# A two-layer graph network on one core: nodes sorted in two groups, queue orders written out by hand

## Chip, core and metric

The kernel runs on one core of a Trainium2 chip. The metric is the device time of one execution in microseconds; nine executions of the kernel before gave a median of 1124.33 us (1121.89 to 1130.77).

The core's engines have a queue each and work through it in order: PE (matrix products), DVE (vector operations), ACT (pointwise functions and scaling), POOL (here almost only DMAs with row indices: gathers and scatters) and SP (plain DMAs).

## The reference

3327 nodes with 512 values each, and an adjacency matrix `adj` of zeros and ones, symmetric, with ones on the diagonal and about 9 neighbours per node. Two layers, each followed by a residual sum and a normalisation of every row:

```python
# layer 0: four heads of 128 columns
feats = einsum('nf,hfo->hno', x, W);  e_s = feats . a_self;  e_n = feats . a_neigh
logits = leaky(e_s[:, :, None] + e_n[:, None, :], 0.2), masked by adj
x = layernorm(x + relu(softmax(logits) @ feats + b))
# layer 1
attn_a = sigmoid(concat[adj @ x, x] @ Wa.T + ba);  attn_b = the same with Wb, bb
h = x @ W_sa
e = where(adj, exp(-leaky(h . a_left + (h . a_right)^T, 0.01)), 0)
x_a = (e / (sum(e) + 1e-5)) @ h
x_b = adj @ (x @ W_gcnb) + b_gcnb
x = layernorm(x + sigmoid(attn_a * x_a + attn_b * x_b))
```

## The kernel before

The matrix has few ones, so the kernel turns it into lists of neighbours and gathers rows. Nodes are handled in tiles of 128 (one per partition), 26 tiles in all. `sparse_pass` does the work; `dense_pass` is a fall-back that a flag calls if a list overflows, and isn't entered here.

**Stage 1, features and lists (lines 129 to 346).** A loop runs over seven chunks of 512 columns (the last has 256). SP loads the chunk of `x` transposed (L213) and the chunk of the matrix in seven loads of up to 1 MB (L218, ten buffers). PE makes the features of each tile (L227, 16 matmuls); ACT copies them out (L232 to L234), POOL writes them to `table0` in DRAM (L235). PE also multiplies the matrix by powers of two (L241, 52 matmuls per chunk), which packs 16 matrix rows into one number; DVE adds the block's number (L247, L250), PE transposes (L256), and DVE finds the largest 24 entries of each node by rounds of eight (`top8`, L50 and L53), takes the bits out in four levels (L261 to L281), sorts them by `top8` again and writes lists and degrees (L285 to L296).

After the last chunk, all nodes are ranked by degree (L301 to L328): a one-hot matrix of degrees, two products with PE, a running sum on DVE. POOL scatters the 26 list tiles to their sorted places (L330), SP loads them back as `srt` (L331). `CAPS` holds how many slots each sorted tile needs: 253 in all, from 23 down to 5.

**Stage 2, layer 0 (L411 to L479).** For each sorted tile `attend` gathers the tile's own rows of `x` (`xg`, L415) and then one row of `table0` for each slot (L382: one POOL instruction gathers 128 rows of 520 numbers). DVE and ACT make the softmax weights (L422 to L437). Each slot's rows are scaled in place, two thirds of the slots by DVE (L446), one third by ACT in four pieces (L444), and PE adds them up by a product with the unit matrix (L451, two instructions per slot). After each group of four tiles the rows are normalised, and `publish` transposes them on PE (L460), makes six columns (L465) and scatters the rows to `table1` (L467). This stage is ordered by a scheduler.

**Stage 3, layer 1 (L482 to L634).** The order is written out by hand: iteration `i` gathers tile `i + 3`, sums tile `i` (weighted on DVE, L544; plain on PE, L561, with some pairs added first by DVE, L546), projects tile `i - 1` (L579) and finishes tile `i - 2`; results are scattered to `out`. Eight gather buffers of six slots.

Every gather and scatter is a POOL instruction, and POOL works strictly in the order of its queue. Layer 0's gathers need `srt` and all of `table0`; layer 1's need all of `table1`.

Of the kernel before, what the change touches and what calls it, by code (L numbers as in the profile page):

```python
# [8 lines left out]
F32 = mybir.dt.float32  # L9
# [11 lines left out]

S = 24
CAPS = (23, 15, 14, 13, 12, 12, 11, 11, 10, 10, 10, 10, 9, 9, 9, 8, 8, 8, 8, 7, 7, 7, 6, 6, 5, 5)
LW = 32
ND = 32
LEVELS = 4
U = 15
U1 = 6
NCOL = 6
# [17 lines left out]
def top8(nc, pool, dst, src, width, tag, i):  # L47

    for r in range(S // 8):
        nc.vector.max(dst[:, 8 * r : 8 * r + 8], src)  # L50
        if 8 * (r + 1) < S:
            rest = pool.tile([P, width], F32, tag=f"top{tag}", name=f"top{tag}{i}_{r}", bufs=3)
            nc.vector.match_replace(rest, dst[:, 8 * r : 8 * r + 8], src, 0.0)  # L53
            src = rest
# [3 lines left out]
def sparse_pass(  # L58
# [27 lines left out]

    nc = tc.nc
# [5 lines left out]
    assert len(CAPS) == NT and NP == N + 1  # L93
    HC = F // 2 + H
    ROW = F + 2 * H

    const = ctx.enter_context(tc.tile_pool(name="const", bufs=1))
# [3 lines left out]
    lists = dram.tile([NP, LW], I32, name="lists")  # L101

    ident = const.tile([P, P], F32, name="ident")
    make_identity(nc, ident)
    ones = const.tile([P, P], F32, name="ones")
    nc.vector.memset(ones, 1.0)
    bias0 = const.tile([P, F], F32, name="bias0")
    nc.scalar.dma_start(bias0, row_bcast(b0, F))
    bias_g = const.tile([P, F], F32, name="bias_g")
    nc.scalar.dma_start(bias_g, row_bcast(b_g, F))  # L110
    bias_ab = const.tile([P, 2], F32, name="bias_ab")
    nc.scalar.dma_start(bias_ab[:, 0:1], row_bcast(ba, 1))
    nc.scalar.dma_start(bias_ab[:, 1:2], row_bcast(bb, 1))

    srt = const.tile([P, NT, LW], I32, name="srt")
    valid = const.tile([P, NT, S], F32, name="valid")
    v1 = const.tile([P, KT, NCOL], F32, name="v1")

    def scatter(group, dst, rows, src, last=None):
# [6 lines left out]
        tc.add_to_no_dep_group(group, put)  # L126


    with tc.tile_pool(name="p0", bufs=1) as p0, tc.tile_pool(name="p0s", bufs=2) as p0s:

        pow2 = p0.tile([P, 4, 32], F32, name="pow2")
        nc.gpsimd.memset(pow2, 0.0)
        pq = p0.tile([P, 8], I32, name="pq")
        nc.gpsimd.iota(pq, pattern=[[-16, 8]], base=0, channel_multiplier=1)
        inside = p0.tile([P, 8], F32, name="inside")
        nc.vector.tensor_scalar(inside, pq, 0, None, ALU.is_ge)
        upto = p0.tile([P, 8], F32, name="upto")
        nc.vector.tensor_scalar(upto, pq, 15, None, ALU.is_le)
        nc.vector.tensor_mul(inside, inside, upto)
        nc.vector.tensor_scalar(pq, pq, 127, None, ALU.add)  # L140
        nc.vector.tensor_scalar(pq, pq, 23, None, ALU.logical_shift_left)
        for s in range(4):
            nc.vector.tensor_mul(pow2[:, s, 8 * s : 8 * s + 8], inside, pq.bitcast(F32))

        pid = p0.tile([P, 4], I32, name="pid")
        nc.gpsimd.iota(pid, pattern=[[0, 4]], base=0, channel_multiplier=1)
        nc.vector.tensor_scalar(pid[:, 1:2], pid[:, 0:1], 7, None, ALU.bitwise_and)
        nc.vector.tensor_scalar(pid[:, 2:3], pid[:, 0:1], 5, 3, ALU.logical_shift_right, ALU.logical_shift_left)
        nc.vector.tensor_scalar(pid[:, 3:4], pid[:, 0:1], 3, 3, ALU.logical_shift_right, ALU.bitwise_and)
        nc.vector.tensor_scalar(pid[:, 3:4], pid[:, 3:4], 5, None, ALU.logical_shift_left)  # L150
# [917 lines left out]
```

## Time and profile before

The profiled execution took 1128.11 us, of which the span from first to last instruction is 1126.4 us.

| from the page | PE | DVE | ACT | POOL |
|---|---|---|---|---|
| busy, us | 840.0 | 718.0 | 225.9 | 657.9 |
| share of the span | 75% | 64% | 20% | 58% |

| stage | from, us | to, us | ended by |
|---|---|---|---|
| features and lists | 0 | 208 | ranks on DVE |
| lists sorted, loaded back | 208 | 250 | first gather of `table0` |
| layer 0 | 250 | 683 | last scatter to `table1`, then the first gather of it |
| layer 1 | 683 | 1126 | last scatter to `out` |

How to read it: the engines' lines give busy time in each stretch; a POOL gather is "busy" only while POOL writes its descriptors, and the rows land some 3.8 us after the issue (the page's part 6). PEclk is the TensorE clock that was granted, as a share of full speed; the DMA share is the mean busy share of the core's 16 DMA engines. "Issue" as the end of an idle stretch means that nothing in the profile shows what ended it.

### The profile page before, as it was taken

What the parts mean: (1) busy time and instruction counts of PE and PEld (TensorE: products, weight loads), DVE (VectorE), ACT (ScalarE), POOL (GpSimd) and SP (SyncE); (2) the same over time, 40 slices, a digit from 0 to 9 for tenths busy, and PEclk for the clock granted to TensorE, in tenths of its full rate; (3) what the DMA queues carried; (4) which work ended last, traced back from release to release, by engine and by line L of the source; (5) the groups of instructions that cost most, each with busy time, mean ns of one, the idle gap of its engine ahead of it and who ended that gap; (6) DMA issues with size and microseconds to landing.
All of it is one profiled execution on the core that took longest, in us unless ns stands there. A gap on an engine that the chain in (4) does not pass through costs nothing. (4 is left out here: it accounts for less than half of the span.)

```text
span 1126.4 us, 10006 instructions
## 1 busy us (share of the span) xinstructions
PE 840.0 (75%) x2662; PEld 427.0 (38%) x2662; DVE 718.0 (64%) x2103; ACT 225.9 (20%) x665; POOL 657.9 (58%) x689
## 2 busy tenths in 40 slices
PE   2999992100897595869867764969898999999981
PEld 0765561000333442425333441424443444444440
DVE  3499889200646355464657543378799898888771
ACT  0111110000423222233222320101212113132321
POOL 3310000457777677777777725777677777777411
PEclk9999996555798598986897885968999999999996
DMA  9999990028777667676767617777667676767400
GB/s 284 392 394 394 394 321 19 7 46 199 219 213 201 177 197 210 198 209 181 211 190 204 198 52 223 197 203 195 184 182 196 186 193 191 195 191 194 139 29 31
DMA packets 87809, 220.71 MB, mean 196 GB/s; under 512 B 17056, under 2 KB 23360, under 8 KB 87744
## 3 DMA queue, kind: packets, MB, share of 16 engines
q0 software_dynamic: 49664, 162.66, 51.1%
q1 hardware_dynamic: 34288, 54.69, 13.6%
q10 hardware_dynamic: 3792, 2.63, 0.8%
q8 instruction: 24, 0.39, 0.1%
q14 instruction: 41, 0.34, 0.1%
HBM read 198.85 MB, written 21.09 MB: 195 GB/s over the span
## 5 line engine op out<-in xcount | busy, mean ns | idle before, releaser
L382 POOL DMA_INDIRECT g<-table,srt x506 | 520.1, 1028 | 165.0 <-issue 138.9
L451 PE MATMUL acc<-g,ident 128*128 128x512 f32 x506 | 255.8, 663 | 88.4 <-DVE g L446 82.2
L561 PE MATMUL acc<-g,ident 128*128 128x512 f32 x378 | 183.3, 624 | 27.5 <-issue 15.2
L451 PEld LDWEIGHTS acc<-g,ident 128*128 128x128 f32 x506 | 104.3, 213 | 223.5 <-issue 140.8
L544 DVE SCALAR_TENSOR_TENSOR sw<-g,e,sw 128x512 f32<-128x512 f32 x227 | 170.2, 750 | 5.8
L446 DVE TENSOR_TENSOR g<-g,w 128x512 f32<-128x512 f32 x178 | 114.3, 692 | 0.7
L227 PE MATMUL pf<-w,xc 128*128 128x260 f32 x416 | 99.6, 394 | 18.7 <-DVE w L194 18.7
L579 PE MATMUL po<-wsa,sT 128*128 128x512 f32 x208 | 100.3, 628 | 15.2 <-ACT sT L572 15.2
L561 PEld LDWEIGHTS acc<-g,ident 128*128 128x128 f32 x378 | 69.6, 199 | 102.8 <-issue 70.6
L422 DVE TENSOR_TENSOR w<-g,srt 128x40 f32<-128x40 f32 (+10 forms) x27 | 5.4, 200 | 152.2 <-DMA g<-table,srt 115.3
L444 ACT ACTIVATE g<-g,w 128x128 f32<-128x128 f32 x300 | 90.5, 388 | 24.1 <-DVE w L437 19.4
L579 PE MATMUL po<-wg,sT 128*128 128x512 f32 x208 | 94.8, 599 | 0.7 <-ACT sT L572 0.7
L227 PEld LDWEIGHTS pf<-w,xc 128*128 128x128 f32 x416 | 79.1, 195 | 36.9 <-DVE w L194 20.5
L235 POOL DMA_DIRECT2D table<-row x26 | 14.1, 544 | 123.6 <-ACT st L234 113.7
L579 PEld LDWEIGHTS po<-wsa,sT 128*128 128x128 f32 x208 | 41.1, 201 | 70.9 <-issue 48.8
L433 ACT ACTIVATE w<-w 128x40 f32<-128x40 f32 (+11 forms) x26 | 6.1, 235 | 303.8 <-DVE w L432 261.5
L572 ACT COPY sT<-pt 128x512 f32<-128x512 f32 x52 | 30.0, 576 | 162.8 <-PE pt L570 162.8
L579 PEld LDWEIGHTS po<-wg,sT 128*128 128x128 f32 x208 | 39.9, 193 | 51.6 <-issue 47.4
L121 POOL DMA_INDIRECT out<-za,srt x26 | 27.0, 1038 | 52.8 <-ACT za L633 46.0
L121 POOL DMA_INDIRECT lists<-st,ranki x26 | 25.3, 972 | 42.9 <-DVE ranki L328 35.3
L121 POOL DMA_INDIRECT table<-x1s,srt x26 | 27.8, 1069 | 35.7 <-ACT x1s L466 29.1
L546 DVE TENSOR_TENSOR g<-g 128x512 f32<-128x512 f32 x64 | 44.3, 692 | 2.2
(152 smaller groups left out, 851.0 us busy)
## 6 DMA issues: line engine op xcount, KB each, us to landing
at<-in_adjT SPq DMA_DIRECT2D x36, 1024.0 KB, 15.3
g<-table,srt POOLq DMA_INDIRECT x506, 3.8
table<-row POOLq DMA_DIRECT2D x26, 260.0 KB, 5.7
xc<-in_xT SPq DMA_DIRECT2D x6, 1024.0 KB, 14.1
at<-in_adjT SPq DMA_DIRECT2D x12, 512.0 KB, 13.3
w<-in_W SPq DMA_DIRECT2D x4, 256.0 KB, 8.1
wsa<-in_W_sa ACTq DMA_DIRECT2D x1, 1024.0 KB, 12.4
wsa<-in_W_sa SPq DMA_DIRECT2D x1, 1024.0 KB, 6.0
```

Source lines behind the costliest of these rows:

```text
L121: put = nc.gpsimd.indirect_dma_start(out=dst, out_offset=bass.IndirectOffsetOnAxis(ap=rows, axis=0), in_=src, in_offset=None, bounds_check ...
L227: nc.tensor.matmul(pf[:, hh, :HC], xc[:, k, (t - t0) * P : (t - t0 + 1) * P], w0[:, k, hh, :], start=(k == 0), stop=(k == KT - 1),)
L235: nc.gpsimd.dma_start(table0[t * P : (t + 1) * P, :], row)
L382: nc.gpsimd.indirect_dma_start(out=g[:, s - s0, :], out_offset=None, in_=table[:, :], in_offset=bass.IndirectOffsetOnAxis(ap=srt[:, j, s : ...
L444: nc.scalar.activation(gv[:, h, :], gv[:, h, :], AF.Copy, scale=w[:, s, h : h + 1])
L446: nc.vector.tensor_tensor(gv, gv, w[:, s, :].rearrange("p (h o) -> p h o", o=1).to_broadcast([P, H, FO]), ALU.mult,)
L451: nc.tensor.matmul(acc, ident, g[:, s - s0, 0:F], start=(s == 0), stop=(s == c - 1))
L544: nc.vector.scalar_tensor_tensor(sw, g[:, i, 0:F], e[:, s : s + 1], sw, ALU.mult, ALU.add)
L546: nc.vector.tensor_add(g[:, i, 0:F], g[:, i - 1, 0:F], g[:, i, 0:F])
L561: nc.tensor.matmul(plain[j], ident, row, start=(not paired and i == 0), stop=(last and i == len(rows) - 1))
L572: nc.scalar.copy(sT, pt)
L579: nc.tensor.matmul(proj[j], sT[:, k, :], wt[:, k, :], start=(half + k == 0), stop=(half + k == KT))
```

## The change

The nodes are put in two groups: the first 12 tiles (three chunks of columns) and the last 14. Each group is ranked, scattered, loaded back and capped by itself; the two lists of slots add up to 126 and 144. The first group's lists are made along with the features of the first 20 tiles, then it is sorted and the remaining features follow. The second group's lists are cut into pieces (`yield`), and layer 0's loop runs three pieces in each of its iterations, between the two halves of the next tile's softmax weights; then come its rank, 14 scatters and the load. The whole of `sparse_pass` is now under a schedule written by hand.

In layer 0 each iteration gathers two tiles ahead, and a tile is normalised and published in four steps that lie in four successive iterations. The bias is added by PE (one more product per tile), the own rows of `x` are gathered into `x1` (12 at once before the first group, then one per tile), the mask of empty slots is replaced by a row of -1e30 in `table0`. The chunks of `x` are loaded by ACT's queue, the matrix by SP in 14 loads of up to 512 KB per chunk with 10 buffers. Block numbers are added by ACT. Both layers share seven gather buffers of six slots. Layer 1 has the same steps with another order of tiles (long and short in turn).

```diff
-CAPS = (23, 15, 14, 13, 12, 12, 11, 11, 10, 10, 10, 10, 9, 9, 9, 8, 8, 8, 8, 7, 7, 7, 6, 6, 5, 5)
+NG = (12, 14)
+CAPS = (23, 14, 12, 11, 10, 10, 9, 9, 8, 7, 7, 6) + (23, 14, 12, 12, 11, 10, 10, 9, 9, 8, 8, 7, 6, 5)
-U = 15
-U1 = 6
+U = 6
+GB = 7
+AT = 10
+PIECES = 3
...
     def scatter(group, dst, rows, src, last=None):
...
+        nc.gpsimd.nop(nofuse=True)
...
+    def list_pieces(i):
...
+        for half, ms in enumerate(halves):
+            for m in ms:
...
+                nc.tensor.matmul(
+                    pc[32 * c : 32 * c + 32, half, :cw], pow2[:, s, :], loaded[i, m],
+                    start=(s == 0), stop=(m + 1 not in ms or s == 3),
+                )
...
+            nc.scalar.activation(
+                v[:rows, half, :cw], pc[:rows, half, :cw], AF.Identity, bias=blk[:rows, half : half + 1]
+            )
...
+        yield
...
+        for j in range(nt):
...
+            top8(nc, p0, ent[:, j, :], pv[:, : P + widths[1]], P + widths[1], "v", t0 + j)
+            if j < nt - 1:
+                yield
...
+        yield
+        for j in range(nt):
+            top8(nc, p0, lst[:, t0 + j, :], cand[:, j].rearrange("p l s -> p (l s)"), LEVELS * S, "c", t0 + j)
...
+        yield
...
+    def sort(g, ranki, queue):
+        for t in range(NG[g]):
+            scatter(f"lists{g}", lists[g][:, :], ranki[:, t : t + 1], st[:, T0[g] + t, :])
+        queue.dma_start(srt[g], lists[g].rearrange("(t p) w -> p t w", p=P))
...
+    more(5)
+    for i in range(NC0):
+        for step, _ in enumerate(list_pieces(i)):
+            more((2, 1, 1, 1, 0, 0)[step])
+    ranki = rank(0)
+    sort(0, ranki, nc.gpsimd)
+    more(NT)
+
+    def later_lists():
+        for i in range(NC0, len(chunks)):
+            yield from list_pieces(i)
+        ranki = rank(1)
+        yield
+        sort(1, ranki, nc.sync)
+        yield
...
+    order0 = first[-2:][::-1] + first[:-2] + list(range(NG[0], NT))
...
+    for j in order0[: NG[0]]:
+        own_x(j)
+    lag = later_lists()
...
+    while i < NT or i == NT or any(todo):
...
+        if i + AHEAD < NT:
+            j = order0[i + AHEAD]
+            if j >= NG[0]:
+                own_x(j)
+            got[j] = gather(table0, j)
+        for j in todo[3]:
+            publish4(j)
...
+        if i < NT:
+            attend(order0[i])
+        if 0 < i <= NT:
...
+            nc.vector.scalar_tensor_tensor(y, accs[j], 0.0, y, ALU.max, ALU.add)
+            done = norm.add(i - 1, y)
...
+        if i + 1 < NT:
+            weigh_a(order0[i + 1])
+        for _ in range(PIECES):
+            next(lag, None)
+        if i + 1 < NT:
+            weigh_b(order0[i + 1])
+        i += 1
...
+    by_len = sorted(range(NT), key=lambda j: CAPS[j])
+    mid = by_len[4:]
+    order = by_len[:2]
+    while mid:
+        order.append(mid.pop())
+        if mid:
+            order.append(mid.pop(0))
+    order += by_len[2:4][::-1]
```

`features(t)` holds the old lines 224 to 235 for one tile, `more(n)` calls it for the next `n` tiles; `rank(g)` holds the old lines 300 to 328 for one group with 25 degrees instead of 32. `weigh_a` is the old lines 421 to 433 up to the exponential without the mask, `weigh_b` the old lines 434 to 437, `attend` the old lines 438 to 451. `publish1` normalises on ACT and transposes on PE, `publish2` copies and makes the columns, `publish3` adds the columns' bias on DVE, `publish4` scatters to `table1`.

## The prediction

> **What bounds the kernel now.** I read first the windows by stage (busy time and instructions of each engine, then granted clock, DMA share, GB/s):
>
> ```profile
> core 0: us, PE busy (x) PEld busy (x) DVE busy (x) ACT busy (x) POOL busy (x), PEclk, DMA share, GB/s
> 28.70:175.00 146.30, 139.78 (x808) 93.74 (x808) 118.51 (x500) 18.77 (x78) 20.78 (x32) 1.00 0.99 367
> 175.00:208.40 33.40, 6.10 (x12) 3.09 (x12) 28.61 (x127) 0.00 (x0) 0.00 (x1) 0.58 0.00 0
> 208.40:249.60 41.20, 0.00 (x0) 0.00 (x0) 2.46 (x8) 0.00 (x0) 26.43 (x28) 0.50 0.11 21
> 249.60:645.90 396.30, 280.62 (x731) 138.90 (x732) 208.67 (x575) 109.44 (x361) 297.23 (x298) 0.81 0.71 200
> 645.90:682.80 36.90, 21.17 (x90) 14.37 (x88) 14.92 (x55) 5.80 (x17) 6.02 (x6) 0.73 0.32 110
> 682.80:1059.00 376.20, 344.99 (x887) 156.23 (x888) 298.23 (x711) 77.08 (x182) 290.73 (x273) 0.93 0.70 192
> ```
>
> Stage 1 is full on PE and DMA. From 175 to 250 one thing at a time works: DVE, then POOL. In both layers POOL issues a gather every 1.3 us almost without a break (298 in 396 us). In layer 1 PE (345 of 376 us) is as near its bound. Next POOL's timeline, which shows the head the change shortens:
>
> ```profile
> 208.40 1.05 POOL L121 DMA_INDIRECT lists<-st,ranki  x1 [35.30 <-DVE ranki L328]
> ...
> 240.32 0.97 POOL L121 DMA_INDIRECT lists<-st,ranki  x1 [0.30 <-issue]
> 248.14 1.12 POOL L415 DMA_INDIRECT xg<-in_x,srt  x1 [6.85 <-issue]
> 249.56 0.97 POOL L382 DMA_INDIRECT g<-table,srt  x1 [0.30 <-issue]
> ```
>
> A scatter takes 1.27 us of the queue; from the start of the last one to the first use of the sorted lists are 7.8 us. Third, the groups of layer 0 with their prices (busy, mean ns | idle before):
>
> ```profile
> L382 POOL DMA_INDIRECT g<-table,srt x249 | 246.4, 990 | 77.1 <-issue 66.4 <-DMA g<-table,srt 7.0 <-PE acc L451 2.8
> L446 DVE TENSOR_TENSOR g<-g,w 128x512 f32<-128x512 f32 x178 | 114.3, 692 | 0.7
> L451 PE MATMUL acc<-g,ident 128*128 128x512 f32 x506 | 255.8, 663 | 88.4 <-DVE g L446 82.2 <-DMA g<-table,srt 6.1
> ```
>
> So a slot costs POOL 1.29 us (0.99 + 0.30), PE 1.01 (255.8/253), and DVE 0.64 (114.3/178) for two slots in three. Last, the list making, in DVE's timeline where the last tile's chain runs alone:
>
> ```profile
> 194.24 0.09 DVE L53 MATCH_VALUE_LOAD topc<-lst,topc 128x8 f32 x1
> 194.32 0.24 DVE L53 MATCH_REPLACE8 topc<-lst,topc 128x96 f32<-128x96 f32 x1
> 194.60 0.26 DVE L50 MAX8 lst<-topc 128x8 f32<-128x96 f32 x1
> 194.89 0.17 DVE L288 COPY ovf<-lst 128x2 f32<-128x2 f32 x1
> ```
>
> Each step needs the one before: starts lie 0.08, 0.28 and 0.29 us apart. A `top8` of 96 values is three such maxima and two replacements, 1.6 us; of 224 values 2.3 (256-wide steps of 0.42 scaled); the four levels of codes 6.4 us for a chunk (26 steps of about 0.25); lists and degrees 1.1. A chunk of four tiles is 4 x 2.3 + 6.4 + 4 x 1.6 + 1.1 = 23 us of DVE in the hand-written order.
>
> **The change, part by part.** All times are in the profiled execution (span 1126.4, device time 1128.1; the runs' median 1124.3 is 0.3% less).
>
> *Head.* PE starts features at about 20 (the row of `a_neigh` that DVE waited for until 11.6 is now first on its queue; then four products and sums of 2.4 us). Before the first ranks PE does 20 tiles of features at 3.5 us (spacing of ACT's copies at 57.3, 60.8, 64.3) = 70, three chunks of L241 at 6.2 = 19 plus 3 us each for the last four loads, which must wait for buffers, = 9, transposes 6: 124. Then the last chunk's DVE chain 16 and the rank 5: 145 (bounds 133 and 157). The later features, PE's, hide behind the sort. Twelve scatters 15.3, wait 7.8: 167. The own rows of twelve tiles stand ahead of the gathers in POOL's queue, 15: first gather at 182 instead of 249.6. That is 67 us gained.
>
> *Layer 0, iterations 0 to 7, beside the second group's lists.* Here I expect the loss. DVE's queue holds, in this order: scaling of tile i, residual and statistics of i-1, `weigh_a` of i+1, three pieces of lists, `weigh_b` of i+1. PE's holds the sums of tile i, then the pieces' L241 products and transposes. So in even iterations DVE's first piece waits until PE has finished tile i (c + 1 products of 1.01 us, the bias among them) and a chunk of products (6.2 alone, 12 if the four late loads land one after another at half the bandwidth; I take 9.5) and ACT and the transposes (1.5). Behind it wait `weigh_b`, thus all scaling of the next tile, thus PE. In odd iterations PE has nothing while DVE makes two `top8`, the codes and the sorting (18.4). Attention starts at 182 + 7.5 + 3.8 (landing) + 1.9 = 195. With slots 6, 7, 23, 14, 12, 11, 10, 10:
>
> i0: 7.1 + 9.5 + 1.5 + 4.6 + 0.7 = 23, to 218. i1: waits for tile 2's 23 gathers (POOL till 228, landed 231.5), then 1.2 + 18.4 + 0.7, to 252. i2: 24.2 + 9.5 + 1.5 + 5.3 = 40.5, to 292. i3: 15.2 + 0.5 + 19.1 = 35, to 327. i4: 13.1 + 16.3 = 29.5, to 357. i5: 12.9 + 0.5 + 19.1 = 32.5, to 389. i6 (half a chunk, two publishing steps): 13.1 + 7 + 10.5 = 30.5, to 420. i7: 13.1 + 6 for the rank: 439, so ranks at about 437.
>
> DVE alone would need 161 of these 242 us (65 scalings 41.6, residuals 12.4, weights 15.2, one norm 2.4, lists and rank 89), which bounds the ranks from below at 356. If the late loads take 12 (+9) and the granted clock falls from 0.81 to 0.65, half way to the idle 0.50 (the 99 us of sums in this walk become 123), they come at 470. I take 437, the walk through the queues. POOL, whose 111 gathers till then would be done by 325, stands still for some 100 us: first for buffers (seven, which three tiles fill), then at the 14 scatters, with all later gathers queued behind them.
>
> *The rest of layer 0* is POOL's: 14 scatters of 1.27, 159 gathers of 1.29, 14 own rows of 1.31, 15 of the publishing scatters at 1.37 = 262. The load of the second list (7.8) hides behind the 15 gathers of the first group's last two tiles (19 us); without them it would stand on the path. The `nop` behind each scatter has no row; from nothing to a 0.3 us gap each, 0 to 12 us over the 40 scatters on this path; nothing is nearest, since the gap exists anyway. The stalls of 29.1 us that POOL had at `table1` scatters vanish into the steps spread over iterations (these rates are without them). The tail: last tile's landing, sums and norm 18, then the publishing queue, one tile per iteration of 2.8 us (copy 0.6, columns 1.24, transposes 0.75, hand-overs), to 33. Then 8 until layer 1's first gather (before: 7.3). 437 + 262 + 33 + 8 = 740, against 682.8.
>
> *Layer 1.* 17 more slots: POOL 17 x 1.37 (1067 ns + 0.30 here) = 23; PE 20 more products of 0.43 = 9 (398 instead of 378 for the unit matrix). The new order puts two tiles of 23 slots at places 2 and 4, and seven buffers hold four of one and two of the tile between, so the second one's gathers wait for the first to end: PE idles some 44 us by the sixth tile, where before it idled 20. Bounds +9 and +27; I take +17 (POOL is nearest to its limit throughout): 461 instead of 443.6.
>
> *Sum.* 740 + 461 = 1201 of span; + 1.7, less 0.3%: 1199.
>
> *Two rules of the skill.* The granted clock is 0.50 where PE idles (208 to 250) and 0.81 in layer 0. The Trainium skill, "TensorE: Matmul & The Clock Gate", Part 1: the gate falls to half rate after an idle window of about 3.4 us and takes as long to open; if each of the eight iterations began cold, 8 x 1.7 us would be an estimated 14 more, 1213. Gathers keep the DMA share at 0.71, loads alone at 0.99. "DMA: Bandwidth & Descriptors", section "Issuing engines are not separate DMA queues", speaks against the change: transfers from all issuing engines interleave on the same 16 DMA engines. By it the 18.7 MB of matrix left at 202 us would get 0.29 of the 370 GB/s beside unbroken gathers, 174 us, and the overlap of the first rival would give 1140 at the earliest.
>
> **The rivals.** *No loss from lists (faster):* if PE and DVE overlap so well that POOL never waits, its queue ends at 182 + 405 (270 gathers, 28 scatters and own rows, 15 publishing scatters), and layer 0 at 628: 628 + 461 = 1089, or 1087. For it: DVE is busy only 209 of 396 us in layer 0. Against: the in-order hand-overs above. It decides from ranks before 362 on, since 362 + 303 (what follows them in layer 0) + 461 is the old span. *DVE alone sets the pace:* ranks at 356, span 1120, 1118: 0.6% less. For it: PE's products may run under DVE's lists. Against: `weigh_b` stands behind the pieces. *Loads starve too:* ranks at 470, 1232. For it: ten buffers hold 10 of a chunk's 14 loads. Against: between two chunks lie 60 us for 6.8 MB. That the overlap isn't made at all is excluded only by the order: the pieces end at iteration 7.
>
> **How the numbers follow.** Chances: serial walk 0.72 (1165 to 1225, the bounds of head and layer 1 on it), DVE's pace 0.12 (1100 to 1160, half of it faster), no loss 0.04, starving 0.12. Faster by over 0.3% (a measurement can't tell less from no change): 0.04 + 0.06 = 0.10; same 0.03; slower 0.87. The range 1135 to 1235 leaves out the fast ends and the worst starving.
>
> **What would show it.** First gather of `table0` near 182; POOL idle for about 100 us before the second group's scatters near 437, DVE waiting for PE's packed products in each even iteration; the last `table1` scatter near 730; layer 1 some 461 us long. If the second scatters come before 362, the prediction is wrong; if after it but layer 1 is no longer than before, its size is.

## The result, and the profile after

The changed kernel takes 1238.29 us (median of 10 runs, 1234.74 to 1243.28) where the kernel before takes 1124.49: 10% more, ratio 1.101 with a 95% interval of 1.099 to 1.103. The forecast was 1199 with a range to 1235; its direction was right, and the time lies 3 us beyond the range. The profiled execution has a span of 1229.9 us, 8.4 below the median.

First the windows of the changed kernel by stage (busy time and instructions of each engine, granted clock, DMA share, GB/s):

```profile
core 0: us, PE busy (x) PEld busy (x) DVE busy (x) ACT busy (x) POOL busy (x), PEclk, DMA share, GB/s
20.00:136.90 116.90, 103.31 (x498) 70.79 (x498) 53.37 (x206) 19.11 (x65) 20.21 (x27) 0.96 0.84 297
136.90:159.90 23.00, 6.47 (x19) 5.03 (x19) 18.39 (x76) 0.63 (x3) 0.58 (x2) 0.63 0.03 12
159.90:201.40 41.50, 20.38 (x86) 16.04 (x84) 0.00 (x0) 4.30 (x18) 28.14 (x33) 0.77 0.38 114
201.40:478.70 277.30, 157.03 (x468) 60.37 (x468) 144.63 (x506) 45.09 (x136) 106.68 (x111) 0.73 0.56 177
478.70:775.80 297.10, 230.75 (x676) 122.00 (x676) 154.48 (x446) 93.30 (x274) 210.05 (x213) 0.83 0.65 187
775.80:1229.90 454.10, 392.63 (x1022) 176.67 (x1022) 350.30 (x844) 91.09 (x208) 314.95 (x296) 0.94 0.64 174
```

The rows are: features and the first group's lists; the end of its lists and ranks, where DVE works almost alone; its sort and own rows, where POOL sets the pace while PE makes the last features; layer 0 beside the second group's lists; the rest of layer 0; layer 1. The fourth is the costly one. In 277 us no engine is busy for more than 157; POOL, which sets the pace later, works for 107.

POOL's timeline shows the borders (start, duration, in brackets the idle time before):

```profile
159.86 1.06 POOL L116 DMA_INDIRECT lists<-st,ranki  x1 [21.57 <-DVE ranki L414]
...
186.18 1.03 POOL L537 DMA_INDIRECT x1a<-in_x,srt  x1 [0.30 <-issue]
...
201.39 0.96 POOL L484 DMA_INDIRECT g<-table,srt  x1 [0.30 <-issue]
...
287.34 1.11 POOL L484 DMA_INDIRECT g<-table,srt  x1 [20.36 <-PE acc L576]
...
438.30 0.96 POOL L484 DMA_INDIRECT g<-table,srt  x1 [0.30 <-issue]
478.73 1.00 POOL L116 DMA_INDIRECT lists<-st,ranki  x1 [39.47 <-DVE den L557]
```

The last line is the second group's first scatter: POOL had stood still for 39.5 us, in front of it for 20.4 (line 287.34) and four times more, 136 us in all. The prices of the groups of layer 0 (busy, mean ns of one | idle time before) hardly moved:

```profile
L484 POOL DMA_INDIRECT g<-table,srt x540 | 547.9, 1015 | 269.2 <-issue 157.5
L576 PE MATMUL acc<-g,ident 128*128 128x512 f32 x540 | 261.7, 644 | 99.2 <-DVE g L573 68.4
L573 DVE TENSOR_TENSOR g<-g,w 128x512 f32<-128x512 f32 x189 | 118.2, 695 | 0.2
```

A gather costs POOL 1.015 us and 0.3 (L484 issues those of both layers; the kernel before had 0.990 in layer 0 and 1.067 in layer 1), and a product 644 ns instead of 663 (695 on average from 201 to 479, 617 behind that). So the added time is in the main waiting, not dearer instructions.

| step | predicted, us | after, us | off by |
|---|---|---|---|
| first list scatter of group one | 145 | 159.9 | +14.9 |
| from there to the first gather of `table0` | 37 | 41.5 | +4.5 |
| from there to group two's first scatter | 255 | 277.3 | +22.3 |
| from there to layer 1's first gather | 303 | 297.1 | -5.9 |
| layer 1 | 461 | 454.1 | -6.9 |
| span | 1201 | 1229.9 | +28.9 |
| median less span | -2 | +8.4 | +10.4 |

### The profile page after: what moved, and what is told of

Its sections match the earlier page's. It is cut to its first block, busy times and chain, and to the rows that moved or that the text cites. A ratio compares the mean times of both kernels' runs of the same rounds, so it can differ in the third digit from the quotient of the medians.

```text
span 1229.9 us, 10517 instructions
## 1 busy us (share of the span) xinstructions
PE 911.8 (74%) x2768; PEld 451.4 (37%) x2768; DVE 733.7 (60%) x2095; ACT 253.5 (21%) x703; POOL 688.0 (56%) x729
## 4 chain that ended last, share of the span: by engine, by line
PE 35%; DVE 18%; DMA 17%; POOL 16%; issue 11%; ACT 2%; SPq 0%; POOLq 0%; DVEq 0%; ACTq 0%
POOL g L484 12%; PE acc L576 11%; DMA g<-table,srt 9%; PE po L755 7%; PE pf L309 5%; PE acc L737 5%; DVE sw L720 5%; DMA at<-in_adjT 4%; POOL lists L116 2%; PE pc L335 2%; PE pcol L592 2%; DVE g L722 1%; DVE ent L54 1%; DVE topv L57 1%; PE acc L565 1%
## 5 line engine op out<-in xcount | busy, mean ns | idle before, releaser
L484 POOL DMA_INDIRECT g<-table,srt x540 | 547.9, 1015 | 269.2 <-issue 157.5
L576 PE MATMUL acc<-g,ident 128*128 128x512 f32 x540 | 261.7, 644 | 99.2 <-DVE g L573 68.4
L737 PE MATMUL acc<-g,ident 128*128 128x512 f32 x398 | 194.6, 626 | 31.1 <-DMA g<-table,srt 16.6
L576 PEld LDWEIGHTS acc<-g,ident 128*128 128x128 f32 x540 | 113.0, 211 | 254.7 <-issue 148.5
L720 DVE SCALAR_TENSOR_TENSOR sw<-g,e,sw 128x512 f32<-128x512 f32 x244 | 182.9, 750 | 6.1
L571 ACT ACTIVATE g<-g,w 128x128 f32<-128x128 f32 x324 | 97.3, 389 | 102.9 <-DVE w L559 102.1
L547 DVE TENSOR_TENSOR w<-g,srt 128x20 f32<-128x20 f32 (+3 forms) x55 | 10.2, 186 | 176.0 <-DMA g<-table,srt 174.7
L737 PEld LDWEIGHTS acc<-g,ident 128*128 128x128 f32 x398 | 72.8, 198 | 114.7 <-issue 53.7
L755 PE MATMUL po<-wsa,sT 128*128 128x512 f32 x208 | 95.8, 604 | 13.8 <-ACT sT L748 13.8
L309 PEld LDWEIGHTS pf<-w,xc 128*128 128x128 f32 x416 | 82.6, 202 | 43.7 <-DVE w L290 20.4
L54 DVE MAX8 ent<-pv 128x8 f32<-128x224 f32 x26 | 10.3, 395 | 146.0 <-PE pv L350 146.0
L592 PE MATMUL pcol<-v,xt 128*128 128x8 f32 x208 | 34.9, 295 | 76.5 <-DVE x1a L595 61.3
L335 PE MATMUL pc<-at,pow 128*32 128x512 f32 (+1 forms) x364 | 62.3, 606 | 27.7 <-DMA at<-in_adjT 22.0
L592 PEld LDWEIGHTS pcol<-v,xt 128*128 128x128 f32 x208 | 34.2, 246 | 91.4 <-ACT xt L589 67.8
L116 POOL DMA_INDIRECT lists<-st,ranki x26 | 26.6, 1023 | 68.4 <-DVE den L557 39.5
```

The costliest lines, as they stand in the source:

```text
L116: put = nc.gpsimd.indirect_dma_start(out=dst, out_offset=bass.IndirectOffsetOnAxis(ap=rows, axis=0), in_=src, in_offset=None, bounds_check ...
L309: nc.tensor.matmul(pf[:, hh, :HC], xc[:, k, o : o + P], w0[:, k, hh, :], start=(k == 0), stop=(k == KT - 1))
L335: nc.tensor.matmul(pc[32 * c : 32 * c + 32, half, :cw], pow2[:, s, :], loaded[i, m], start=(s == 0), stop=(m + 1 not in ms or s == 3),)
L484: nc.gpsimd.indirect_dma_start(out=buf[:, s - s0, :], out_offset=None, in_=table[:, :], in_offset=bass.IndirectOffsetOnAxis(ap=srt[g][:, i ...
L571: nc.scalar.activation(gv[:, h, :], gv[:, h, :], AF.Copy, scale=w[:, s, h : h + 1])
L576: nc.tensor.matmul(acc, ident, buf[:, s - s0, 0:F], start=False, stop=(s == CAPS[j] - 1))
```

## The experiments

In the first three sets of runs (e1 to e4; the control and e6; e5 and e7) the kernel before took 1242 to 1247 us; in the later sets 1123 to 1126. Ratios are always to the kernel before in the same set. The control, c_after, says what the changed kernel does in the first sets:

> The changed kernel unaltered, as a control beside the other runs on this chip. Every theory expects the ratio of 1.10 to the kernel before that was measured for it; where the chip is slower than the first one, as that of the first four experiments was (1246.5 us for the kernel before), the ratio shows whether the changed kernel loses more or less there.

Measured: 1368.81 us, ratio 1.0985 (1.0895 to 1.1075): the loss is the same share there. Its second group's first scatter came at 515.8 instead of 478.7.

### Where the lists stand

All pieces in the first iteration (e2_lists_first):

```diff
-PIECES = 3
+PIECES = 24
```

> All 24 list pieces in iteration 0: after the first tile's sums nothing of the first group's attention runs until the second group's lists are made. Theory (the lists beside the attention cost more than the lists alone, since each piece holds up weights, scaling and sums in DVE's and PE's queues, and POOL stands still for buffers): lists from 222 to about 326, the second group's scatters near 327 instead of 479, then POOL without a break; layer 1's first gather near 717 instead of 775.8; time 1165 to 1195. Rival (overlap hides something, so that giving it up costs the attention that was hidden): the attention of eight tiles, some 92 slots, comes on top, time 1240 or more.

Measured: 1307.38 us, ratio 1.051 (1.044 to 1.058), scatters at 347.8, 168 us before the control's. By the two ratios to the kernel before that is 4.3% less than the changed kernel: not overlapping is better than overlapping in this order. The rival, whose 1240 us would be a ratio of 1.10 or more, is out. This run was not repeated in the later sets, where ACT's long waits (last section) are absent.

All pieces ahead of the attention, in the time in which POOL sorts (e3_sort_shadow, and e3b_sort_shadow in a later set):

```diff
-    ranki = rank(0)
+    more(4)
+    ranki = rank(0)
...
     lag = later_lists()
+    for _ in range(23):
+        next(lag)
```

> All pieces and the second ranks stand before the attention's loop, so that DVE and PE make the second group's lists while POOL sorts the first group, fetches its own rows and the first 36 gathers (DVE idles there from 159 to 212 in the changed kernel); four of the last six feature tiles go to PE while it waits for the first ranks. Theory: four chunks at DVE's 23 us each from 171, ranks of group two near 258, its scatters 258 to 276, then POOL at 1.27 us an instruction until 610, layer 1's first gather near 648, time 1095 to 1125: at or below the kernel before. Rival (layer 0's pipeline or the split itself costs the time, wherever the lists are): still above 1180.

> The experiment with all lists ahead of the attention again. Theory as before: second group's scatters near 258 instead of 478.7, layer 1's first gather near 648 instead of 775.8, time 1095 to 1125, ratio 0.975 to 1.0 on a chip where the kernel before takes 1124. Rival (the split costs more than the sort's shadow gives, as 17 slots alone cost 4.4%): ratio above 1.005.

Measured: 1262.3 us and ratio 1.017 (1.010 to 1.025) in the first set, 1134.78 us and 1.0070 (1.0049 to 1.0091) in the later one, scatters at 278.0, layer 1's first gather at 676.8, a span of 1134.3. From the first gather to the second scatters pass 74 us instead of 277; the sums of eight tiles then come behind, and 96 us of the span are had back. But the rival of the second run holds: even so the split doesn't gain on the kernel before. The expected 258 for the scatters was missed by 20, and what follows them took 399 us instead of 390.

### What holds the iterations

PE's and ACT's part of a piece ahead of the tile's sums, DVE's part where it was (e6_pe_ahead, e6b_pe_ahead). Of the two `next(lag, None)` in an iteration the first issues products and transposes, the second maxima, codes and sorting; the pieces are divided anew for it, in lines that aren't printed:

```diff
+        next(lag, None)
         if i < NT:
             attend(order0[i])
...
-        for _ in range(PIECES):
-            next(lag, None)
+        next(lag, None)
```

> PE's and ACT's part of each list piece (packed products, transposes) is issued ahead of the sums of the tile, DVE's part stays where it was: the second tile pair's transposes and the next chunk's products run while DVE is at the lists and the scaling before them. Theory (serial walk through the queues: DVE's first piece of an even iteration waits for PE's sums and the chunk's products, 21 to 29 us each): these waits of DVE shrink to below 5 us, a pair of iterations takes some 45 us instead of 64, 81 and 68, the second group's scatters come near 400 instead of 479, and the time falls to 1150 to 1185 where the kernel before takes 1124 (ratio 1.02 to 1.055). Rival (DVE's own work of 161 us is not the issue, but loads are: late loads and gathers share the DMA): the products just wait ahead of the sums instead of behind them, scatters after 455, ratio above 1.08.

> The experiment with PE's part of the pieces ahead of the sums again. Theory: pairs of iterations of 45 to 50 us instead of 64, 81 and 68, scatters at 400 to 420 instead of 478.7, ratio 1.02 to 1.05. Rival (late loads now stand ahead of the sums): scatters after 440, ratio above 1.06.

Measured: ratio 1.029 (1.017 to 1.041) in the first sets, 1.038 (1.036 to 1.040) and 1170.05 us in the later one; scatters at 409.6. Two lists of waits (what waited for what: total, times, longest), of the changed kernel and of this one:

```profile
DVE ent L54 <- PE pv L350: 146.0, 18, 34.9
```
```profile
DVE ent L54 <- PE pv L353: 51.8, 12, 34.0
```

DVE's wait for the transposes fell from 146 to 52 us, 34 of which is one wait in the head; in layer 0's iterations alone it was 93.7 us in six waits and is gone. This part of the theory holds as forecast: the same work, issued in another order, takes 75 us less up to the second scatters (202.7 instead of 277.3). PE now waits 58 us for ACT's copy `v` of the products. 38.5 of them lie ahead of the first sums, where `v` (at 219.1) stands behind an exponential (at 219.0) that waits for gathered rows; in the changed kernel PE is idle there for 30.8 us too.

DVE's `weigh_b` ahead of the pieces (e5_weigh_b_first):

```diff
+        if i + 1 < NT:
+            weigh_b(order0[i + 1])
         for _ in range(PIECES):
             next(lag, None)
-        if i + 1 < NT:
-            weigh_b(order0[i + 1])
```

> weigh_b of the next tile stands before the three list pieces in DVE's queue instead of behind them. Theory (what holds the attention is that DVE's scaling of the next tile, and so PE's first sum, stands behind the pieces; and the pieces behind PE's products): only ACT's third of the scaling comes earlier, the second group's scatters stay within 8 us of the control's 515.7 and the ratio to the kernel before at 1.085 to 1.105. Rival (the prediction's own words, that it is weigh_b behind the pieces that holds all scaling): scatters 30 us earlier or more, ratio below 1.07.

Measured, in two executions only: ratio 1.088 (1.076 to 1.099), scatters at 506.4, 9.4 us before the control's: 1.4 more than the theory allowed, far from the rival's 30. So it isn't `weigh_b` that holds the attention. That the scaling waits for its own place behind the pieces is what remains by the order of the queue; no run moved it alone.

Fourteen buffers for the matrix, at the price of one gather buffer (e1_late_loads, e1b_late_loads):

```diff
-GB = 7
-AT = 10
+GB = 6
+AT = 14
```

> Fourteen buffers for the matrix instead of ten (all 14 loads of a chunk lie ahead of its products), paid for with six gather buffers instead of seven. Theory (the products of a chunk were mis-sized because four late loads arrive 3.6 us apart beside the gathers): the products of L335 in iterations 0, 2 and 4 take 6 to 7 us instead of 15.5, 16.8 and 17.3, the half chunk some 5 instead of 9.2, the three chunks of the head some 3.5 less each; the second group's first list scatter comes 35 to 45 us earlier than 478.7, and the time is 1190 to 1215 (the lost gather buffer takes some of it back). Rival (the bandwidth is what is short, more buffers only move the wait): products of 12 us or more and a time of 1230 or more. Rival (DVE's lists alone hold the iterations): the products get shorter, the iterations don't, 1230 or more.

> The experiment with fourteen buffers again, on a chip where the kernel before takes 1124 us if one is to be had (on the slower chips ACT's waits of 15 to 38 us beside the gathers hid the loads). Theory (late loads mis-sized the products of a chunk): L335 takes 6 to 7 us in iterations 0, 2 and 4 instead of 15.5, 16.8 and 17.3, the first ranks come 7 us earlier, the second group's scatters at 435 to 450 instead of 478.7, ratio 1.06 to 1.08. Rival (bandwidth, not buffers): products of 12 us or more, scatters after 465. Rival (DVE's pieces alone set the iterations): products short, scatters after 465 all the same.

Measured: ratio 1.081 (1.075 to 1.087) against the control's 1.0985 in the first sets, where ACT's waits hid the loads (scatters at 501.2); 1225.56 us and 1.088 (1.085 to 1.090) in the later one. There PE's timeline shows the term alone. The changed kernel, iteration 0:

```profile
222.87 3.64 PE L335 MATMUL pc<-at,pow 128*32 128x512 f32 x32
227.34 1.06 PE L335 MATMUL pc<-at,pow 128*32 128x512 f32 x6 [0.83 <-ACT v L340]
229.33 1.73 PE L335 MATMUL pc<-at,pow 128*32 128x512 f32 x6 [0.93 <-DMA at<-in_adjT]
232.86 1.05 PE L335 MATMUL pc<-at,pow 128*32 128x512 f32 x4 [1.80 <-DMA at<-in_adjT]
236.71 1.74 PE L335 MATMUL pc<-at,pow 128*32 128x512 f32 x4 [2.80 <-DMA at<-in_adjT]
238.38 0.47 PE L350 MATMUL pv<-ident,v 128*128 128x128 f32 x1
```

The same chunk with fourteen buffers:

```profile
216.51 3.64 PE L335 MATMUL pc<-at,pow 128*32 128x512 f32 x32
220.98 3.63 PE L335 MATMUL pc<-at,pow 128*32 128x512 f32 x20 [0.83 <-ACT v L340]
224.54 0.33 PE L350 MATMUL pv<-ident,v 128*128 128x128 f32 x1
```

With ten buffers the products run to 228.4 and then wait for loads that could only be issued when the first buffers came free; of four late loads (the second is of half size) the first lands at 229.3, the last at 236.7. With fourteen the chunk takes 8.1 us from its first product to the end of its last instead of 15.6; in iterations 2, 4 and 6 it takes 8.1, 8.1 and 4.5 instead of 16.8, 17.4 and 9.2: 30 us in all. The second scatters come at 449.7, 29 us earlier (6.2 of them in the head), as forecast; the chunk and the ratio lie beyond their forecasts of 6 to 7 us and 1.06 to 1.08.

What the chunk loses isn't all on the path. Iteration 0 is 7.4 us shorter here (22.7 instead of 30.2 from sum to sum), and iteration 1 is longer by as much (41.1 instead of 33.2): in both kernels it waits for the last of tile 2's 23 gathers. DVE's first use of that gather, in the changed kernel and with fourteen buffers:

```profile
258.11 0.18 DVE L547 TENSOR_TENSOR w<-g,srt 128x20 f32<-128x20 f32 x1 [7.80 <-DMA g<-table,srt]
```
```profile
252.34 0.18 DVE L547 TENSOR_TENSOR w<-g,srt 128x20 f32<-128x20 f32 x1 [10.32 <-DMA g<-table,srt]
```

Both lie 57 us behind POOL's first gather of `table0` (201.4 and 195.2). POOL issued the gathers up to that last one without a break and started it at 245.9 and 239.4; it landed 12 to 13 us later, where the median of the first gathers is 3.8. Iterations 2, 4 and 6 gain 8.9, 8.8 and 5.0 us. The time falls by only 1.2%, because the lost gather buffer costs 5 us in the rest of layer 0 (302.1 instead of 297.1) and 18 in layer 1 (472.0 instead of 454.1).

### The head

The eight small loads behind five tiles of features on ACT's queue (e4_small_loads):

```diff
-                nc.scalar.dma_start(v1[:, :, 3 * s + 1 + i], src)
-    nc.scalar.dma_start(bias0, row_bcast(b0, F))
...
     more(5)
+                nc.scalar.dma_start(v1[:, :, 3 * s + 1 + i], src)
+    nc.scalar.dma_start(bias0, row_bcast(b0, F))
...
```

> The eight small loads (four vectors, two rows, two scalars) leave the front of ACT's queue and are issued after five tiles of features. Theory (ACT's first copy waited behind these issues until 34.9, so PE idled 7 us from 29.9 to 36.9, and the list products and thus the matrix's loads began that much later): PE's idle time before the sixth tile vanishes, the first ranks come 6 to 9 us earlier than 159.9 and the time falls by as much, to 1228 to 1234. Rival (DVE or the matrix's loads bound the head): first ranks within 2 us of 159.9, no change of the time.

Measured: ratio 1.084 (1.076 to 1.093), first ranks at 157.5 instead of the control's 160.3. PE's timeline in this kernel:

```profile
21.14 20.13 PE L300 MATMUL pf<-w,xc 128*128 128x260 f32 x78 [3.54 <-DVE w L281]
41.21 3.64 PE L326 MATMUL pc<-at,pow 128*32 128x512 f32 x32
51.66 6.51 PE L326 MATMUL pc<-at,pow 128*32 128x512 f32 x20 [6.81 <-ACT v L331]
```

The gap ahead of the sixth tile is gone, and in its place PE waits 6.8 us for ACT's first `v`, which now stands behind the same issues. Neither theory: the issues cost some 7 us wherever they stand ahead of something that PE needs.

Lists first in the head (two tiles of features at its start, three a chunk), the small loads on POOL's queue, all lists ahead of the attention (e7_head_reordered):

```diff
-    more(5)
+    more(2)
...
-            more((2, 1, 1, 1, 0, 0)[step])
+            more((2, 1, 0, 0, 0, 0)[step])
+    more(4)
     ranki = rank(0)
...
```

> All second-group lists before the attention, and a head that makes lists first: two tiles of features before the first chunk's products instead of five, three a chunk instead of five, the rest behind the first sort; the eight small loads on POOL's queue. Theory (POOL's queue from its first gather on is the floor, 397 us for layer 0 without a wait; everything that holds up that first gather, or stops POOL for buffers, is paid in full): first list scatter 118 to 128 instead of 160, first gather of features 175 to 187 instead of 201, second group's scatters 225 to 260, and a time below the kernel before, ratio 0.95 to 0.99. Rival (features, not lists, set the first gather, since all 26 tiles must be in the table): first gather after 195, ratio 1.0 to 1.02 as in the experiment with the lists in the sort's shadow.

Measured: 1255.4 and 1268.8 us in the two faster of four runs, against 1242.46: about 1.017, no gain over the 1.017 of its simpler form (its runs gave no interval). The first scatter came at 131.3, but the first gather of `table0` only at 216.7 (203 there): the rival's gather came. All 26 tiles of features have to be in the table; PE finished them at 196.8, then came the last write to the table and, from 201.5 on, the twelve own rows.

### The slots, the split, layer 1

The kernel before once more (c_before), and the kernel before with the 270 slots of the changed one (e8_17_slots):

```diff
-CAPS = (23, 15, 14, 13, 12, 12, 11, 11, 10, 10, 10, 10, 9, 9, 9, 8, 8, 8, 8, 7, 7, 7, 6, 6, 5, 5)
+CAPS = (23, 23, 14, 14, 12, 12, 12, 11, 11, 10, 10, 10, 10, 9, 9, 9, 9, 8, 8, 8, 7, 7, 7, 6, 6, 5)
```

> The kernel before, unaltered, for its trace on a chip like those of the experiments, where it takes 1242 to 1247 us instead of 1124. Expected if the chips merely run their gathers slower: POOL's spacing of gathers above 1.29 us throughout. Expected if other engines are held up while gathers run, as ACT was for 37.7 us in the control: waits of ACT, DVE and PE whose input is long there, in both layers, some 120 us in all.

> The kernel before with the 270 slots of the changed kernel (its one list of 26 capacities replaced by the sorted 26 of both groups; the 17 slots added gather the empty row), nothing else. Theory: layer 0 is POOL's, so 17 x 1.29 = 22 us there, and layer 1 is PE's, so 17 to 20 more products, 6 to 10 us: ratio 1.023 to 1.03. Rival (POOL's queue sets both layers, as the prediction took for layer 1): 17 x 1.29 + 17 x 1.37 = 45 us, ratio 1.04. Rival (the slots vanish in waits that are there anyway): below 1.015.

Measured: 1125.0 us for the first, the time of the first measurement, so it shows nothing of what lengthened the first three sets; 1171.02 us for the second, ratio 1.044 (1.038 to 1.049). Windows of layers 0 and 1 of the kernel before in this set, then with 17 slots more:

```profile
249.20:678.40 429.20, 301.08 (x820) 153.06 (x820) 223.89 (x629) 115.27 (x378) 303.43 (x305) 0.81 0.67 194
678.40:1123.30 444.90, 386.24 (x1002) 175.55 (x1002) 333.25 (x814) 90.59 (x208) 296.06 (x279) 0.93 0.59 167
```
```profile
249.00:719.00 470.00, 326.96 (x854) 164.04 (x854) 232.42 (x640) 122.47 (x402) 320.59 (x322) 0.79 0.66 187
719.00:1172.90 453.90, 396.45 (x1022) 178.71 (x1022) 351.88 (x844) 90.74 (x208) 315.94 (x296) 0.94 0.63 174
```

Layer 1 gets 9.0 us longer, as PE's products make it (396.5 busy instead of 386.2), not POOL's 23. Layer 0 gets 40.8 longer, not 22. Of the 19 beyond POOL's 17 instructions, 12.1 us are waits of POOL for sums of PE to free a buffer, under 3 in the kernel before; the rest isn't accounted for. The ratio is the first rival's 1.04, for another reason. The price holds for the gather buffers of the kernel before, three of 15 slots in layer 0; in the changed kernel's layer 0 it wasn't measured.

One group with the 253 slots of the kernel before, the rest of the changed kernel's layer 0 and layer 1 kept (e10_one_group):

```diff
-NG = (12, 14)
+NG = (26,)
...
-    for j in order0[: NG[0]]:
-        own_x(j)
...
-            if j >= NG[0]:
-                own_x(j)
+            own_x(j)
```

> The changed kernel's layer 0 as a pipeline, its queues and its layer 1, but one group: all lists first, one sort of 26 scatters, the 253 slots of the kernel before; each tile's own rows fetched ahead of its gathers; features spread four a chunk behind the lists. Theory (the split is what costs, the pipeline gains): the stalls of 29 us that POOL had at the scatters into the second table are gone and nothing stands beside the attention, so 20 to 40 us less than the kernel before, ratio 0.965 to 0.985. Rival (the pipeline or the hand-written order costs as well): ratio 1.0 or more.

Then with a head in which the next chunk's products stand ahead of this chunk's codes and sorting (e11_one_group_head, e11b_one_group_head), and with its last features ahead of the ranks (e13_one_group_best). e11 also has fourteen buffers for the matrix and the small loads on POOL's queue; its diff shows what else differs from e10, that of e13 what differs from e11:

```diff
-        for step, _ in enumerate(list_pieces(i)):
-            more((2, 1, 1, 0, 0, 0)[step])
-    more(NT)
...
+        for _ in range(nt):
+            next(parts)
...
+            next(following)
+        for _ in parts:
+            pass
...
+        more(3)
     ranki = rank(0)
+    more(1)
     sort(0, ranki, nc.gpsimd)
+    more(NT)
```

```diff
-        more(3)
+        more(3 if i < len(chunks) - 1 else NT)
     ranki = rank(0)
-    more(1)
     sort(0, ranki, nc.gpsimd)
-    more(NT)
```

> One group as in the last experiment, with a head that lets DVE run through: the next chunk's products stand ahead of the codes and the sorting of this one, three tiles of features a chunk, fourteen buffers for the matrix, the small loads on POOL's queue. Theory (that run lost its gain of 13 us in layer 0 and 11 us in layer 1 in the head, whose first scatter came at 230 instead of 208): DVE's 23 us a chunk from 40 on, first scatter 190 to 202, first gather 235 to 248, layer 0 416 and layer 1 434 as there; 1080 to 1100 us, ratio 0.962 to 0.98, faster than both kernels. Rival (the head is PE's or the loads', not DVE's): first scatter after 215, ratio 0.99 or more.

> The one-group kernel with the reordered head, with its last five feature tiles ahead of the ranks, in PE's 6 us of idle time there, instead of three ahead and two behind. Theory (the table's last rows, written behind the sort at 252.7 to 259 in that run, stood ahead of POOL's first own row): from the first list scatter to the first gather 41 us as in the kernel before instead of 46, the first scatter no more than 2 us later: 3 to 6 us less, ratio 0.988 to 0.991. Rival (PE's products delay the ranks by as much): 0.993 to 0.996.

> The one-group kernel with the reordered head once more, with more executions, since its first ratio of 0.9938 and the 0.9993 of its variation lie closer than chips do. Theory (the gain is there: 14 us in layer 0 and 8 us in layer 1 against 14 us lost ahead of the first gather): 0.990 to 0.997, its interval below 1. Rival (no difference): an interval that holds 1.

Measured: 1127.33 us, ratio 1.0044 (1.0015 to 1.0072) for the first; 1119.63 us, 0.9938 (0.9918 to 0.9958), and again 1118.4 us, 0.9946 (0.9920 to 0.9971) for the second; 1122.73 us, 0.9993 (0.9972 to 1.0014) for the third.

In the first kernel layer 0 took 416.0 us and layer 1 434.0, 13 and 11 less than in the kernel before, but its first list scatter came at 230.2 instead of 208.2; the ratio is its rival's. The second is faster than both kernels, by half a per cent and not by the 2 to 4 expected. Windows of its sort, layer 0 and layer 1:

```profile
216.80:263.00 46.20, 7.22 (x26) 4.62 (x24) 0.00 (x0) 1.56 (x6) 29.56 (x32) 0.59 0.16 38
263.00:678.40 415.40, 317.11 (x870) 161.25 (x870) 214.51 (x604) 126.00 (x378) 299.06 (x304) 0.84 0.71 201
678.40:1114.80 436.40, 384.99 (x1002) 174.69 (x1002) 332.95 (x814) 90.84 (x208) 297.57 (x279) 0.93 0.62 171
```

In this kernel layer 0 takes 415.4 us instead of 429.2 and layer 1 436.4 instead of 444.9. But its first scatter comes at 216.8 (208.2 in the kernel before) and its first gather 46.2 us later (41.0 there): the rival's numbers came (first scatter after 215, ratio 0.99 or more), though DVE is busy for 143 of the 187 us from 30 on. In the third kernel the first scatter moved to 220.2, and the first gather followed 47.4 us later, not the 41 that the theory expected: that the table's last rows held up POOL's first own row is refuted. Its ratio lies beyond even its rival's 0.993 to 0.996.

Layer 1 in the kernel before's order of tiles (e12_layer1_order):

```diff
-    by_len = sorted(range(NT), key=lambda j: CAPS[j])
-    mid = by_len[4:]
-    order = by_len[:2]
...
+    down = sorted(range(NT), key=lambda j: -CAPS[j])
+    order = [down[k] for k in [NT - 1, NT - 2, NT - 3, 0, NT - 4, 1, NT - 5] + list(range(2, NT - 5))]
```

> The changed kernel with the kernel before's order of tiles in layer 1 (three short tiles, then the longest ones between short ones, the rest downward) in place of the one that takes a long and a short tile in turn. Layer 1 from its first gather to the end takes 454.1 us in the changed kernel, 443.6 and 444.9 in the kernel before, 453.9 there with 17 slots more, and 434.0 and 436.4 with one group in the changed kernel's layer 1. Theory (the new order gains some 10 us, which the 17 slots, worth some 20 here, more than take back): layer 1 462 to 468 us, ratio 1.105 to 1.115. Rival (the order changes nothing; the prediction took it as a loss of 10): 452 to 456, ratio 1.099 to 1.103. Rival (the prediction's own step, that the new order costs): below 450.

Measured: ratio 1.101 (1.098 to 1.104), layer 1 459.5 us instead of 454.1. That lies between theory and first rival, and the time shows no difference. The prediction's step, that the new order costs time over the whole layer, is out.

## Why the prediction was right, and where it failed

**Direction and mechanism.** The walk through the queues was right: ranks of group two long after the break-even of 362, DVE waiting for PE in each even iteration, POOL idle, now 136 us instead of "some 100". Its reason that `weigh_b` stands behind the pieces isn't what holds: moved ahead of them it gave 9.4 us (e5). The experiments that move list pieces (1.051, 1.007 and 1.038 instead of 1.10) show that their place in the queues is what costs, and e8 shows that 17 slots cost 47 us in the kernel before by themselves. "No loss" and "DVE's pace" fell.

**The step that failed: "12 if the four late loads land one after another at half the bandwidth; I take 9.5".** Neither value nor bound held; the chunks took 15.6, 16.8, 17.4 and 9.2 (the half one). Half of the prediction's 370 GB/s gives the four late loads (1.84 MB) 9.9 us; from the issue of the first to the landing of the last they took 12.7, 13.8 and 14.4. Most of the excess lies in the first one: it landed 5.3, 5.5 and 7.6 us after its issue, where its bytes at half the bandwidth make 2.8. The three behind it (1.31 MB) came in 7.4, 8.3 and 6.8 us, 158 to 193 GB/s, about the half. In the head, where no gathers run, the first takes 4.2 to 4.9 us and the three behind it 3.4 to 4.2. The queues (packets, MB, share of the 16 engines) from 229.3 to 236.7, where the chunk of iteration 0 waits, gathers first, then loads:

```profile
q0 software_dynamic: 474, 1.57, 55.3%
q1 hardware_dynamic: 694, 1.34, 48.3%
```

The Trainium skill, "DMA: Bandwidth & Descriptors", section "Issuing engines are not separate DMA queues", says that all transfers interleave on the same engines; the trace agrees: loads and gathers move side by side, nearly half each, and a gather lands up to 12.3 us after its start instead of 3.8.

On the path the miss is in iterations 2, 4 and 6, the later ones of those with products: 46.8, 36.9 and 36.1 us where the walk had 40.5, 29.5 and 30.5, in all 19.3 of the 22.3 that were missing. The others but the first two came out near the walk: 33.8, 30.9 and 15.6 where it had 35, 32.5 and 17. DVE's lists in iteration 1 took 17.9 where it had 18.4. Iterations 0 and 1 took 30.2 and 33.2 instead of 23 and 34, 6.4 too long together, and here a second step failed: tile 2's gathers "landed 231.5", 49.5 us behind the first gather's start at 182. Measured were 56.7 (201.4 to 258.1), since the last one landed 12.2 us after its own start. So the first chunk's 15.6 us is hidden behind that wait, as the run with fourteen buffers shows, and that iteration 1 alone agrees is chance.

"Loads starve too", at 470, was the rival that named the cause; I gave it 0.12. That its 470 is near the 478.7 is chance too: 24 of its 33 us were a slower clock, and the first gather came 19 us later than it assumed.

**The head, 19 us.** PE ended the first group's transposes at 136.9 instead of 124: 7.0 us it waited for ACT's first copies (ACT's queue first held the small loads), 3 us more for the three chunks' late loads, 1 for a later start. The chain on DVE and the ranks took 23 instead of 21. Behind the scatters, the table writes of the last feature tiles and of the single row stood in POOL's queue until 185.9 ahead of the own rows, which the sum had left out: 4.5.

**The rest of layer 0** held as a sum: 297 instead of 303 us. The stalls at the second table's scatters did not all vanish: POOL was idle for 3.7 us before the first group's twelve, but for 24.2 before the second group's fourteen, nearly all of it behind the last gather at 737.2. That tail, to layer 1's first gather, was 38.6 against 33 and 8; in the kernel before it was 38.2, and 21.5 of the 29 us of stalls lay in it too.

**Layer 1, "I take +17 (POOL is nearest to its limit throughout)".** It came out +10.5, a net of two things that the sum didn't part. With 253 slots the changed kernel's layer 1 took 434.0 to 437.1 us (e10, e11, e11b, e13), so 17 slots cost 17 to 20 us there, and the rest of the new layer 1 gained 8 to 10 on the kernel before. That +10.5 is near the lower bound of +9 is chance. From 895 us on PE is busy 306.7 of 334.9 us and POOL 225.0, so PE is nearer to its limit than POOL. Of the "44 us" of idle time at its start 33 came (119.2 us less 85.9 busy up to 895; 28.7 with the kernel before's order), and the rest of the layer gave them back.

**The clock.** The granted clock was 0.73 in the iterations, and each of the eight did begin at half of it. Two windows of iteration 0, columns as in the windows of the section on the result:

```profile
215.30:219.60 4.30, 4.30 (x5) 1.78 (x6) 1.80 (x4) 1.74 (x6) 3.38 (x4) 0.50 0.70 195
219.60:222.30 2.70, 2.70 (x7) 1.25 (x6) 0.56 (x3) 0.00 (x0) 2.09 (x3) 0.95 0.81 203
```

The first five products come 0.85 us apart at a granted clock of 0.50, the next ones some 0.43 apart at 0.95. The 186 products of the iterations took 98.6 us of PE's time where 0.43 each would make 80. That is some 18 us, of the size of the 14 estimated from the Trainium skill, "TensorE: Matmul & The Clock Gate", Part 1, and the trace agrees with the half rate. They did not come on top: the price of 1.01 us a slot, taken from layer 0 of the kernel before at a clock of 0.81, holds such stretches already (the walk's sums of 99 us against 98.6).

**The median.** 10.4 us of the miss lie outside the trace: the profiled execution of the changed kernel is shorter than its median, that of the kernel before was longer.

## What to carry to other kernels

Work that is to run "beside" other work in queues that keep their order runs beside it only where neither stands in front of what the other waits for; issue the producer's part ahead (here PE's products ahead of the sums, 59 us of the span) before counting on an idle engine. A load whose buffer comes free only when its consumer starts is on the path from its issue to its landing beside the other transfers (here 5.3 to 7.6 us for the first 512 KB), not for its bytes alone; cost it so, and the gathers beside it too. And price a split by what it adds everywhere: 17 slots in 253 cost the kernel before 4.4%, and the split with its lists ahead of the attention (1.007) lost to the same queues with one group (0.994), though their heads differ too.

## What the runs showed of the hardware that was not expected

In the first three sets ACT, PE and SP stood still for tens of us while their input was ready and POOL issued gathers. ACT's timeline in the changed kernel, as first measured and as the control:

```profile
222.55 0.23 ACT L552 ACTIVATE w<-w 128x28 f32<-128x28 f32 x1 [5.51 <-DVE w L551]
226.60 0.69 ACT L340 ACTIVATE v<-pc,blk 128x512 f32<-128x512 f32 x1 [3.83 <-PE pc L335]
```
```profile
223.81 0.23 ACT L552 ACTIVATE w<-w 128x28 f32<-128x28 f32 x1 [5.46 <-DVE w L551]
261.77 0.69 ACT L340 ACTIVATE v<-pc,blk 128x512 f32<-128x512 f32 x1 [37.73 <-remote]
```

In both PE's first half of the chunk ended 3.6 us after its start (at 226.5 and 227.1). In the control ACT took it up 34.7 us later, after POOL's gathers had paused (the last of the row began at 253.5); "remote" means that the profile shows no releaser. SP issued two loads of the matrix at 235.6 and 246.1 there and the next eleven in 10.9 us from 257.3 on. The kernel before took 11% longer in these sets and the changed one 10.5%; that such waits make this up is likely but not shown, and what causes them stays open: the kernel before left no trace in those sets.
